# The KAN's input product on four 32-column strips, with its values copied onto the inner parts by transfers through DRAM

## The chip, the cores and the metric

The kernel runs on one core of one Trainium2 chip, as one launch. The metric is the device time of a whole execution in microseconds; the time before is 1592.74 us, the median of three runs (1592.62 to 1594.12). Besides, one execution was profiled. A core has five instruction streams that run side by side and wait for each other by semaphores: TensorE (PE, with its weight loads PEld), VectorE (DVE), ScalarE (ACT), GpSimd (POOL), and SyncE (SP), which in this kernel only issues transfers (DMAs). Each stream runs strictly in its own order: whatever waits at its head holds up all that stands behind it.

## The reference, cut to what matters

There are 16 batch rows of 512 tokens with 128 features. Six residual layers follow each other, each on the layer-normed `x`: half a KAN, causal attention with 16 heads, half a KAN, half a mixture of experts, a linear recurrence, half a mixture of experts. The change concerns the KAN, which is computed twice for each row, with the same weights, so 32 times:

```python
s = jnp.einsum('btd,dm->btm', x, Win) + bin_          # M = 64 middle features
h = jax.nn.relu(s[..., None] * W1 + b1)               # each with INNER = 16 inner functions
g = jnp.einsum('btmh,mh->btm', h, W2) + b2
out = jnp.einsum('btm,md->btd', g, Wout) + bout
```

So each of the 64 middle features is scaled, shifted and cut at zero in 16 ways, and the 16 results are added up with weights.

## The kernel before

Tokens of one row lie along the free dimension (512 of them). The 64 middle features are taken in two halves of 32. On the 128 partitions stand four copies of one half, one for each of four inner parts (partition = part times 32 + feature), and each inner part has four inner functions. One ACT instruction (`kan_h`, L377) with a scale and a bias for each partition therefore makes 4 times 32 of the relu values for all tokens; eight of them, four to a half, make all 1024.

To have the same 32 values on four groups of partitions, the kernel before keeps the input weights four times side by side (`win`, 128 x 2 x 4 x 32) and lets one 128x512 matmul per half (`ps_s`, L358) compute each value four times. ACT copies the result out of PSUM to `kan_s0` and `kan_s1` (L361). Then come the eight `kan_h`, eight matmuls of 32 output partitions (`ps_kg`, L387) which sum over the inner functions, a copy (`kan_g`, L393), the output product (`ps_ko`, L401), and the add to `x` on DVE (L402).

Buffers: `kan_s0` has two (and shares them with `kan_g` and others), `kan_s1` has one. The flag `kan_held` keeps a second KAN from writing `kan_s1` before the first has released it. Two PSUM banks, `mm`, are lent by `bank()` to all side work.

What sets the order: the kernel is a set of Python generators, which a planner steps turn by turn (`turn()`). What is emitted in one turn goes into the streams of PE, ACT, DVE and POOL in that order and stays there. Copies out of PSUM are put off to the next turn (`later`, `flush`). While `paced` is set, each turn has a budget for each engine (`MOST`), and a generator that asks for more than is left (`need`, or `bank` with its `work`) waits for a later turn. SP's order isn't written by hand: a scheduler places the transfers by when it estimates their data to be ready.

The main loop has one stage for each row (44 turns): in it `weights(b)` makes the exponentials of row b (`ps_st` L713 on PE, `pt` L716 on ACT, masks L718 on POOL), `maxima(b + 1)` the scores of the next row for their maxima (`ps_sc` L649, DVE L654 and L659), and `outputs` the product with the values (`ps_av` L739). Beside them run as side work `stage_out(b - 1)` (output product, second KAN, gate) and `stage_in(b + 4)` (first KAN, then `attn_in`, which makes the queries and keys of that row). `attn_in` writes the parts of queries and keys to DRAM (`qs` L427, `ks` L434) and reads them back onto the partitions of the scores (`qp` L516, `kp` L510); row maxima go the same way (`ms` L688, `qp` L690). All these are SP's.

Before the first stage the rows 0, 1 and 2 go through their first KAN, rows 0 and 1 through `attn_in` (`first`, `second`, `forward`), while SP loads weights and all of `x`. After the last stage come the experts (L1026, L1039, L990) with the recurrences as side work; the last two second KANs, of rows 14 and 15, run into that time.

The matmuls of fp32 are split in the records into two: a product of 512 columns shows as two instructions.

Of the kernel before, what the change touches and what calls it, by code (L numbers as in the profile page):

```python
# [8 lines left out]
F32 = mybir.dt.float32  # L9
# [8 lines left out]
P = 128  # L18
S = 512
NT = S // P  # L20
D = 128
M = 64
MH = M // 2
NI = 4
# [12 lines left out]
GB = 8  # L37
IN, OUT = 38, 8
LATE = 28
EP = 5  # L40
PLACES = 8
AHEAD = 4
# [6 lines left out]
def tile_macaron(  # L49
# [9 lines left out]
    nc = tc.nc  # L59
# [45 lines left out]
    with ExitStack() as ph:  # L105
# [17 lines left out]

        center = w1p.tile([D, D], F32, name="center", tag="yT")
        nc.vector.tensor_scalar_add(center, ident, -1.0 / D)
        win = cst.tile([D, 2, NI, MH], F32, name="win")
        binc = cst.tile([P, 2], F32, name="binc")
        kw1 = cst.tile([P, 2, NV], F32, name="kw1")
        kb1 = cst.tile([P, 2, NV], F32, name="kb1")
# [4 lines left out]
                rows = src[half * MH : (half + 1) * MH, :]  # L134
                nc.scalar.dma_start(out=dst[:, half, :], in_=rows.rearrange("m (i v) -> i m v", i=NI))

        for half in range(2):
            cols = win_in[:, half * MH : (half + 1) * MH]
            nc.sync.dma_start(out=win[:, half, :, :], in_=cols.unsqueeze(1).to_broadcast([D, NI, MH]))
        inner(kw1, kw1_in)  # L140
        for half in range(2):
            rows = bin_in[half * MH : (half + 1) * MH]
# [102 lines left out]
        def take(**work):  # L245

            for e, w in work.items():
                room[e] -= w
# [8 lines left out]
                yield  # L257

        held, kan_held, hurry = [0], [0], [False]

        def bank(shape, dtype, name, work=0.0):


            while held[0] == 2 or (paced[0] and work > room["pe"]):
                yield
            room["pe"] -= work
            held[0] += 1
            return mm.tile(shape, dtype, name=name, tag="mm")

        def freed():  # L270
            held[0] -= 1
# [26 lines left out]
        def norm(xt, name="kan_xT", pool=None, whole=False):  # L298

            st = small.tile([P, NT, 6], F32, name="ln_st")  # L300
            mv = small.tile([P, NT, 2], F32, name="ln_mv")
            for c in range(NT):
                if c % 2 == 0:
                    yield from need(dve=0.55)
                nc.vector.bn_stats(out=st[:, c, :], in_=xt[:, c, :])
            yield
            yield from need(dve=0.6, pool=1.4)
            for c in range(NT):
                nc.vector.bn_aggr(out=mv[:, c, :], in_=st[:, c, :])  # L309
            rstd = small.tile([P, NT], F32, name="ln_rstd")  # L310
            nc.gpsimd.tensor_scalar_add(rstd, mv[:, :, 1], EPS)  # L311
            nc.gpsimd.tensor_tensor(rstd, rstd, mhalf, ALU.pow)  # L312
            yield
            yield
            yield
            yield from rest(1)
            xl = w2p.tile([P, NT, D], F32, name="kan_x")
            if whole:
                for c in range(NT):
                    if c % 2 == 0:  # L320
                        yield from need(dve=0.85)
# [27 lines left out]
        def kan(b):  # L349

            _, xT = yield from norm(x[b])
            sk = []
            for half in range(2):
                while half and kan_held[0]:
                    yield
                kan_held[0] |= half
                ps = yield from bank([P, S], F32, "ps_s", 0.9)
                nc.tensor.matmul(ps, lhsT=win[:, half, :, :].rearrange("d i m -> d (i m)"), rhs=xT,  # L358
                                 start=True, stop=True)
                sh = (w1p if half else w2p).tile([P, S], F32, name=f"kan_s{half}")  # L360
                later.append(lambda sh=sh, ps=ps: nc.scalar.copy(sh, ps))  # L361
                yield
                take(act=0.6)
                freed()
                sk.append(sh)
            yield

            hs = []
            begin = now[0]
            U = 2 * NV  # L370
            for t in range(U):
                while now[0] < begin + 15 * t // 8:
                    yield
                yield from need(act=0.8, **({"pool": 1.25} if t == 1 else {}))
                half, v = t // 2 % 2, t // 4 * 2 + t % 2
                h = hp.tile([P, S], F32, name="kan_h")
                nc.scalar.activation(h, sk[half], AF.Relu, bias=rbias[:, half, v : v + 1],  # L377
                                     scale=kw1[:, half, v : v + 1])
                hs.append((half, v, h))
                if t == 1:  # L380
                    nc.gpsimd.tensor_tensor(x[b], x[b], kcst.unsqueeze(1).to_broadcast([P, NT, D]), ALU.add)
                yield
            pg = yield from bank([P, S], F32, "ps_kg", 1.0)
            for begins in (True, False):
                for half, v, h in hs[0:4] if begins else hs[4:8]:
                    o = half * M + v % 2 * MH
                    nc.tensor.matmul(pg[o : o + MH, :], lhsT=w2d[:, half, v, :], rhs=h,  # L387
                                     start=begins, stop=not begins)
                if begins:
                    yield  # L390
                    yield from need(pe=1.0)
            gT = w2p.tile([P, S], F32, name="kan_g", tag="kan_s0")
            later.append(lambda: nc.scalar.copy(gT, pg))  # L393
            kan_held[0] = 0
            yield
            take(act=0.6)
            freed()
            yield
            po = yield from bank([P, NT, D], F32, "ps_ko", 0.9)
            for c in range(NT):  # L400
# [119 lines left out]
        def centered(ps, w, to=None):  # L520

            ps = ps[:, 0 : w.shape[1]]
            nc.tensor.matmul(ps, lhsT=center, rhs=w, start=True, stop=True)
            if to is None:
                nc.vector.tensor_copy(w, ps)
            else:
                nc.vector.tensor_copy(to, ps.rearrange("k (h d) -> k d h", d=HD))

        def center_win():
            psc = yield from bank([P, 2 * NI * MH], F32, "ps_kc0")  # L530
            centered(psc, win.rearrange("d a i m -> d (a i m)"))
            freed()

        def cleared(pack):
# [777 lines left out]
```

## Time and profile before

| | |
|---|---|
| median of 3 runs | 1592.74 us (1592.62 to 1594.12) |
| profiled execution, whole time | 1585.11 us |
| its span | 1583.1 us |
| mean granted clock of PE | 0.984 |
| first scores (L649) | 67.9 us after the span's start |
| `ps_s` products (L358) | 71.1 us of PE in 128 records, 644 ns each |
| copies to `kan_s` (L361) | 64, 586 ns each |
| `kan_h` (L377) | 256, 821 ns each |
| `ps_kg` (L387) | 512 records on strips of 32 columns |
| SP's transfers in all | 67.7 MB on its queue, DMA engines busy 15% for it |

The profile has one execution, so all stretches of time below are of that one, which is 7.6 us shorter than the median. Its view of busy times gives each engine's share, which adds up to more than the span, since the engines overlap. What counts is the chain of work that ended last: it is followed back from the last instruction, at each step to what released it or to the instruction before it on its engine. Where a line has its time in that chain, shortening it shortens the whole, until something else ends last. The view of instructions in order of time shows start, duration, engine, line and count; what stands there in brackets is the idle time before an instruction and what ended it.

### The profile page before, as it was taken

The page shows a single profiled execution, that of the slowest core. Times are in us where ns is not written, and L with a number is a line of the kernel's source. Part 1 is how long each engine was busy: PE and PEld are TensorE (multiplying, and loading weights), DVE is VectorE, ACT ScalarE, POOL GpSimd, SP SyncE. Part 2 cuts the span into 40 slices and gives each one's busy share as a digit, 9 for nine tenths or more (in the row PEclk, how much of TensorE's full clock was granted, in tenths as well). Part 3 has the DMA queues.
Part 4 walks back from the last instruction along what each step waited for, and adds up shares of the span by engine and source line. Part 5 has one row for each costly group of instructions (what it writes and reads, how often), then busy time and mean ns, then how long its engine had stood idle before and what let it go on. Part 6 is the DMA issues. An engine that isn't in the chain of part 4 may idle for free.

```text
span 1583.1 us, 33175 instructions
## 1 busy us (share of the span) xinstructions
PE 1479.8 (93%) x11902; PEld 1045.6 (66%) x11905; DVE 1085.0 (69%) x3574; ACT 960.5 (61%) x1852; POOL 922.7 (58%) x1439
## 2 busy tenths in 40 slices
PE   4689989999999999999999899999999999999997
PEld 2334454455445454445444489999998999999997
DVE  5587877878788788888888345765569665753333
ACT  3445767777778777777776865444454444544443
POOL 2535545555555564556454766667666666767773
PEclk9889999999999999999999999999999999999998
DMA  5220110122111210221122113223332332333332
GB/s 136 81 58 30 58 52 13 50 59 60 36 33 53 60 52 12 58 60 35 30 79 68 50 45 70 60 57 73 72 73 59 72 72 63 81 64 67 69 67 60
DMA packets 107466, 92.87 MB, mean 59 GB/s; under 512 B 23469, under 2 KB 95862, under 8 KB 107062
## 3 DMA queue, kind: packets, MB, share of 16 engines
q1 hardware_dynamic: 84464, 67.67, 15.0%
q0 software_dynamic: 21584, 22.89, 7.8%
q8 instruction: 93, 1.52, 0.4%
q14 instruction: 71, 0.58, 0.1%
q10 hardware_dynamic: 1254, 0.20, 0.1%
HBM read 59.20 MB, written 35.45 MB: 60 GB/s over the span
## 4 chain that ended last, share of the span: by engine, by line
PE 76%; DVE 10%; ACT 7%; issue 2%; DMA 2%; POOL 1%; SPq 1%; ACTq 0%; DVEq 0%; POOLq 0%
PE ps_h L1026 13%; PE ps_y L1039 13%; PE ps_av L739 9%; PE ps_st L713 7%; PE ps_sc L649 5%; PE acc L990 5%; PE ps_kg L387 4%; ACT pt L716 4%; PE ps_s L358 3%; DVE below L654 3%; ACT kan_h L377 2%; PE ps_t L338 2%; PE ps_x L955 2%; DVE topped L659 2%; PE ps_g L800 2%
## 5 line engine op out<-in xcount | busy, mean ns | idle before, releaser
L716 ACT ACTIVATE pt<-ps_st 128x512 f32<-128x512 f32 x682 | 369.9, 566 | 126.3 <-PE ps_st L713 124.6
L718 POOL TENSOR_SCALAR_AFFINE_SELECT pt<-pt 128x128 f32<-128x128 f32 (+2 forms) x704 | 250.9, 365 | 320.4 <-ACT pt L716 314.4
L654 DVE CUSTOM_DVE_ANT_0 below<-ps_sc,causal 128x512 bf16<-128x512 f32 (+1 forms) x512 | 315.6, 616 | 106.5 <-PE ps_sc L649 91.0
L935 POOL DMA_INDIRECT xg<-xnd,tokI x256 | 252.8, 988 | 82.9 <-issue 37.8
L1028 ACT ACTIVATE mo<-ps_h 128x512 f32<-128x512 f32 x256 | 152.8, 597 | 217.7 <-PE ps_h L1026 217.4
L713 PE MATMUL ps_st<-qp,kp 128*128 128x512 bf16 (+1 forms) x990 | 247.6, 301 | 33.2 <-ACT pt L716 30.7
L1026 PE MATMUL ps_h<-xin,mw 128*128 128x128 f32 x2048 | 272.5, 276 | 0.0
L1039 PE MATMUL ps_y<-mw,mo 128*128 128x128 f32 x2048 | 270.8, 275 | 0.0
L649 PE MATMUL ps_sc<-kp,qp 96*128 96x512 bf16 (+3 forms) x1024 | 256.6, 304 | 5.9 <-DVE topped L654 3.9
L1026 PEld LDWEIGHTS ps_h<-xin,mw 128*128 128x128 f32 x2048 | 250.3, 192 | 12.4 <-issue 9.9
L1039 PEld LDWEIGHTS ps_y<-mw,mo 128*128 128x128 f32 x2048 | 249.4, 192 | 1.0 <-DVE ye L1036 0.8
L713 PEld LDWEIGHTS <-kp 128*128 128x128 bf16 x1024 | 94.9, 100 | 183.9 <-issue 164.7
L377 ACT ACTIVATE kan_h<-kan_s,rbias,kw 128x512 f32<-128x512 f32 x256 | 207.6, 821 | 0.0
L1056 POOL DMA_INDIRECT sum<-mo,tokI x93 | 152.1, 1635 | 69.7 <-issue 26.7
L739 PE MATMUL ps_av<-pt,va 128*32 128x512 f32 (+3 forms) x2048 | 164.6, 439 | 1.0 <-POOL pt L718 0.7
L649 PEld LDWEIGHTS <-qp 96*128 96x128 bf16 x1024 | 95.9, 99 | 87.4 <-issue 64.7
L659 DVE TENSOR_REDUCE topped<-ps_sc 128x2 f32<-128x512 f32 (+1 forms) x192 | 127.0, 683 | 23.1 <-PE ps_sc L649 22.8
L739 PEld LDWEIGHTS ps_av<-pt,va 128*32 128x32 f32 x2048 | 53.3, 109 | 85.4 <-issue 42.7
L312 POOL TENSOR_TENSOR ln_rstd<-ln_rstd,mhalf 128x4 f32<-128x4 f32 x96 | 102.4, 1067 | 8.0
L311 POOL TENSOR_SCALAR ln_rstd<-ln_mv 128x4 f32<-128x4 f32 x96 | 21.9, 228 | 138.1 <-DVE ln_mv L309 137.7
L1045 DVE SCALAR_TENSOR_TENSOR ye<-ps_y,gainT,ye 128x128 fp32r<-128x128 f32 x83 | 29.0, 349 | 84.7 <-ACT ye L1042 84.4
L1045 DVE SCALAR_TENSOR_TENSOR parts<-ps_y,gainT,parts 128x128 fp32r<-128x128 f32 x80 | 27.9, 349 | 83.9 <-ACT parts L1042 83.8
(204 smaller groups left out, 2296.5 us busy)
## 6 DMA issues: line engine op xcount, KB each, us to landing
qp<-qs SPq DMA_DIRECT2D x64, 288.0 KB
xnd<-kan_x SPq DMA_DIRECT2D x32, 256.0 KB
sum<-x SPq DMA_DIRECT2D x62, 128.0 KB
qs<-qpart SPq DMA_DIRECT2D x48, 128.0 KB
kp<-ks SPq DMA_DIRECT2D x48, 96.0 KB
x<-in_L_attn_x_dram SPq DMA_DIRECT2D x16, 256.0 KB
mw<-in_L_ffn_w_dram SPq DMA_DIRECT2D x16, 256.0 KB
xg<-xnd,tokI POOLq DMA_INDIRECT x256, 2.5
```

What stands on the lines that cost most here:

```text
L377: nc.scalar.activation(h, sk[half], AF.Relu, bias=rbias[:, half, v : v + 1], scale=kw1[:, half, v : v + 1])
L649: nc.tensor.matmul(v[:, u, 0:n], lhsT=qp[r][0:MXR, g, bass.ts(c, P)], rhs=kp[0:MXR, r, 0:n], start=alone, stop=(u == len(gs) - 1), skip_gr ...
L654: nc.vector.tensor_tensor_reduce(below[:, 0:n], v[:, 0, 0:n], causal[:, S - n : S], 1.0, LOWEST, ALU.add, ALU.max, accum_out=maxs[:, h, c ...
L659: nc.vector.tensor_reduce(maxs[:, h : h + len(gs), c], v[:, :, 0:n], AX.X, ALU.max)
L713: nc.tensor.matmul(v[:, u, 0:n], lhsT=kp[ROWS, r, bass.ts(c, P)], rhs=qp[r][ROWS, g, c * P : S], start=True, stop=True)
L716: nc.scalar.activation(o, v[:, :, 0:n], AF.Exp, scale=HD ** -0.5)
L718: nc.gpsimd.affine_select(out=dg, in_=dg, compare_op=ALU.is_ge, fill=0.0, base=0, pattern=[[0, len(gs)], [1, P]], channel_multiplier=-1)
L739: nc.tensor.matmul(po[32 * g : 32 * g + 32, c * P : S], lhsT=va[:, c, r, :], rhs=pt[:, g, OFF[c] : OFF[c] + n], start=(c == 0 and not odd) ...
L935: nc.gpsimd.indirect_dma_start(out=xgs[i // E % 2][:, i % E, :], out_offset=None, in_=xnd[b], in_offset=bass.IndirectOffsetOnAxis(ap=tokI[ ...
L1026: nc.tensor.matmul(pst[:, f, :], lhsT=mw1[e][:, bass.ts(f, P)], rhs=xins[i // E % 2][:, i % E, :], start=True, stop=True)
L1028: nc.scalar.activation(hs[u], pst, AF.Gelu)
L1039: nc.tensor.matmul(py, lhsT=hs[u][:, f, :], rhs=mw2[e][:, f, :], start=(f == 0), stop=(f == NF - 1))
```

## The change

`win` is kept once (128 x 64). The product is made once: four matmuls, each of 32 output partitions and 256 tokens, write the two halves of features and the two halves of tokens on four strips of one PSUM bank. ACT copies 256 columns to `kan_m`. Two transfers write it to a DRAM tile `kn` of 64 features by 512 tokens, and two transfers read from that tile, one for each half of features, four times over onto the four groups of partitions of `kan_s0` and `kan_s1`. The flag `kan_held` is taken before both reads, not between the two halves. Between the reads and the first `kan_h` the generator rests three turns (`REST`).

```diff
-        win = cst.tile([D, 2, NI, MH], F32, name="win")
+        win = cst.tile([D, M], F32, name="win")
...
+        nc.sync.dma_start(out=win, in_=win_in)
...
             _, xT = yield from norm(x[b])
+            ps = yield from bank([P, S // 2], F32, "ps_s", 0.75)
+            for half in range(2):
+                for th in range(2):
+                    o = th * M + half * MH
+                    nc.tensor.matmul(ps[o : o + MH, :], lhsT=win[:, half * MH : (half + 1) * MH],
+                                     rhs=xT[:, th * S // 2 : (th + 1) * S // 2], start=True, stop=True)
+            sm = w1p.tile([P, S // 2], F32, name="kan_m")
+            later.append(lambda: nc.scalar.copy(sm, ps))
+            yield
+            take(act=0.4)
+            freed()
+            scr = tc.dram_tile([2, MH, S], F32, name=f"kn{len(kns)}")
+            kns.append(scr)
+            for th in range(2):
+                nc.sync.dma_start(out=scr.rearrange("a m t -> (a m) t")[:, th * S // 2 : (th + 1) * S // 2],
+                                  in_=sm[th * M : (th + 1) * M, :])
+            yield
+            while kan_held[0]:
+                yield
+            kan_held[0] = 1
+            yield
             sk = []
             for half in range(2):
-                while half and kan_held[0]:
-                    yield
-                kan_held[0] |= half
-                ps = yield from bank([P, S], F32, "ps_s", 0.9)
-                nc.tensor.matmul(ps, lhsT=win[:, half, :, :].rearrange("d i m -> d (i m)"), rhs=xT,
-                                 start=True, stop=True)
                 sh = (w1p if half else w2p).tile([P, S], F32, name=f"kan_s{half}")
-                later.append(lambda sh=sh, ps=ps: nc.scalar.copy(sh, ps))
-                yield
-                take(act=0.6)
-                freed()
+                nc.sync.dma_start(out=sh, in_=scr[half].unsqueeze(0).to_broadcast([NI, MH, S]))
                 sk.append(sh)
-            yield
+            for _ in range(REST):
+                yield
```

The product that centers `win` (`center_win`) becomes 64 columns wide instead of 256.

More of the change, by code (lines that the diff above doesn't have):

```diff
@@ L39 @@
 LATE = 28
+REST = 3
 EP = 5
@@ L135, in inner @@
                 nc.scalar.dma_start(out=dst[:, half, :], in_=rows.rearrange("m (i v) -> i m v", i=NI))
-        for half in range(2):
-            cols = win_in[:, half * MH : (half + 1) * MH]
-            nc.sync.dma_start(out=win[:, half, :, :], in_=cols.unsqueeze(1).to_broadcast([D, NI, MH]))
+        nc.sync.dma_start(out=win, in_=win_in)
         inner(kw1, kw1_in)
@@ L259, in tile_macaron @@
         held, kan_held, hurry = [0], [0], [False]
+        kns = []
         def bank(shape, dtype, name, work=0.0):
@@ L351, in kan @@
             _, xT = yield from norm(x[b])
+            ps = yield from bank([P, S // 2], F32, "ps_s", 0.75)
[19 more added lines that the diff above has]
+            yield
             sk = []
             for half in range(2):
-                while half and kan_held[0]:
-                    yield
-                kan_held[0] |= half
-                ps = yield from bank([P, S], F32, "ps_s", 0.9)
-                nc.tensor.matmul(ps, lhsT=win[:, half, :, :].rearrange("d i m -> d (i m)"), rhs=xT,
-                                 start=True, stop=True)
                 sh = (w1p if half else w2p).tile([P, S], F32, name=f"kan_s{half}")
-                later.append(lambda sh=sh, ps=ps: nc.scalar.copy(sh, ps))
+                nc.sync.dma_start(out=sh, in_=scr[half].unsqueeze(0).to_broadcast([NI, MH, S]))
+                sk.append(sh)
+            for _ in range(REST):
                 yield
-                take(act=0.6)
-                freed()
-                sk.append(sh)
-            yield
             hs = []
@@ L529, in center_win @@
         def center_win():
-            psc = yield from bank([P, 2 * NI * MH], F32, "ps_kc0")
-            centered(psc, win.rearrange("d a i m -> d (a i m)"))
+            psc = yield from bank([P, M], F32, "ps_kc0")
+            centered(psc, win)
             freed()
```

## The prediction

> **What bounds the kernel now.** The page first: its chain of work that ended last, then its times by engine.
>
> ```profile
> span 1583.1 us, 33175 instructions
> PE 1479.8 (93%) x11902; PEld 1045.6 (66%) x11905; DVE 1085.0 (69%) x3574; ACT 960.5 (61%) x1852; POOL 922.7 (58%) x1439
> PE 76%; DVE 10%; ACT 7%; issue 2%; DMA 2%; POOL 1%; SPq 1%; ACTq 0%; DVEq 0%; POOLq 0%
> PE ps_h L1026 13%; PE ps_y L1039 13%; PE ps_av L739 9%; PE ps_st L713 7%; PE ps_sc L649 5%; PE acc L990 5%; PE ps_kg L387 4%; ACT pt L716 4%; PE ps_s L358 3%; DVE below L654 3%; ACT kan_h L377 2%; PE ps_t L338 2%; PE ps_x L955 2%; DVE topped L659 2%; PE ps_g L800 2%
> ```
>
> PE carries the chain, and the product that the change rewrites (ps_s, L358) lies on it with 3% of the span. Busy times by stretch say how closely PE binds during attention; columns are PE, PEld, DVE, ACT, POOL busy, granted clock, DMA share, GB/s:
>
> ```profile
> 468.00:520.00 52.00, 49.64 (x400) 25.34 (x396) 42.56 (x141) 41.29 (x77) 29.75 (x64) 1.00 0.16 46
> ```
>
> PE is busy 95%, DVE 82%, ACT 79%: what PE saves is mostly saved, until ACT or DVE takes over. DMA engines are idle 84%. The chain in order of time prices one KAN (start, us, what; x2 is one matmul, which the records split in two):
>
> ```profile
> 441.02 0.99 PE ps_av L739 x8
> 443.43 1.43 PE ps_av L739 x24
> ...
> 448.59 0.98 PE ps_s L358 x2
> ...
> 451.34 0.88 PE ps_s L358 x2
> 452.24 0.58 ACT kan_s L361
> ```
>
> Last, the instructions in order of time at the start, SP's queue and ACT (start, us, count):
>
> ```profile
> 24.28 5.70 SPq L195 DMA_DIRECT2D wo<-in_L_attn_Wo_dram  x8
> 30.08 1.17 SPq L217 DMA_DIRECT2D wlam<-in_L_attn_W_lam_dram  x2
> 31.30 0.58 SPq L219 DMA_DIRECT2D wf<-in_L_attn_W_F_dram  x1
> 31.93 1.11 SPq L1082 DMA_DIRECT2D wst<-in_L_attn_W_fromP_dram  x2
> ```
>
> ```profile
> 17.23 0.59 ACT L361 COPY kan_s<-ps_s 128x512 f32<-128x512 f32 x1 [2.17 <-PE ps_s L358]
> 18.75 0.58 ACT L361 COPY kan_s<-ps_s 128x512 f32<-128x512 f32 x1 [0.94 <-PE ps_s L358]
> 19.24 5.75 ACT L377 ACTIVATE kan_h<-kan_s,rbias,kw 128x512 f32<-128x512 f32 x8
> ```
>
> The first KAN has its input at 17-19 us, while SP issues loads until 32. Today the KAN needs nothing from SP.
>
> The sum is made against this execution: 1585.1 us, span 1583.1 and 2.0 around it. The median of the three runs shown is 1592.7, 7.6 above; I add the change to that.
>
> **The change, part by part.** There are 32 KANs (two for each of 16 batch rows). In the built orders the planner's turns are 3 more (1613 against 1610), all of them before the first scores; each attention stage keeps its 44 turns, about 1.18 us each (52 us by 44).
>
> *1. Product and copies (removed, added).* Two 128x512 products cost 0.98 + 0.88 = 1.86 us of chain. The four 32x256 products stand on four strips, as ps_av's do: eight records of 512 columns took 0.99, 24 records of 384, 256 and 128 columns 1.43, so a group of 256 about 0.48. After strip work the next ps_st stands with 0.27-0.32 in the chain instead of 0.22; I allow 0.2 for going into strips and back. PE saves 1.1-1.2 per KAN. ACT's two 0.585 copies become one of 256 columns (L957's took 0.37): 0.8 saved. 27 KANs lie in PE-bound attention stages (not the first five: three precede the scores, two fall into the stage whose pace DVE's score maxima set). PE: 27 x 1.15 = 31, of which I take 80%, since ACT and DVE are close behind: 25. ACT, on about a fifth of that stage's chain (pt 11.0%, kan_h 6.1%, copies): 27 x 0.8 x 0.18 = 4. Together **-29**; ends -38 (all of PE's, plus ACT's and the bubbles) and -15 (half of PE's).
>
> The page "TensorEngine Tiling (Array Packing)", Key Properties, of the Trainium skill speaks against this part: changing the tiling mode drains TensorE. It gives no price; the 0.05-0.1 us after strip groups above is what the chain shows of it.
>
> *2. The first KANs (a new wait).* In the built order of SP's queue the first KAN's two writes stand behind all the loads above, up to wf. So they issue at about 31.4 and 32.0 instead of the value being there at 18. Small writes land 2.0-2.3 us after issue (the trace's completion records of ks and qs), so the first broadcast read issues at 34.1; an unhurried 256 KB read lands after 2.7-3.0 (x<-sum). ACT's first kan_h: about 37 instead of 19.2. It stands at the head of ACT's queue, and PE's ps_kg behind it stands ahead of the transposes of the next two KANs, so rows 1 and 2 don't fill the gap. DVE's clearing of buffers does part of it. Then: kan(0) +14 at its add, row 0's rope +13; kan(1) may read only once kan(0) released its buffers, +12 at its end; kan(2)'s second read issues behind row 0's four query loads (4 x 288 KB and 288 KB of keys, of which the last landed 6.3 us after issue before) and lands near 75; ACT's kan_xT of row 1 stands behind the kan_h that waits for it (58.2 before, 77 now). PE's first scores follow row 1's products and kan(2)'s ps_kg and ps_ko: 67.9 before, 86 now. Nothing later has slack to take this back. **+18.5**; ends 13 (only the 13 seen at row 0's rope) and 22.
>
> *3. Steady state: do the reads come in time?* After the copy: two writes (issue about 0.55 each), 2.0 to land, a read at 2.9, there at 5.7 on idle queues. REST and the other yields place the first kan_h five turns after the copy where nothing else holds it (5.9 - 0.37 = 5.5 us), seven or more in most KANs. So most wait 0-0.3: nothing taken. Not so where SP has row b-1's query loads at that moment. In the built queue the reads of the first KANs of rows 8, 10 and 12 stand behind two key writes, three qp loads and three kp loads. Before, those took this:
>
> ```profile
> 478.46 0.54 SPq L434 DMA_DIRECT2D ks<-kpart  x1
> 479.37 0.82 SPq L516 DMA_DIRECT2D qp<-qs  x1
> 480.58 2.06 SPq L510 DMA_DIRECT2D kp<-ks  x3
> 482.68 1.58 SPq L516 DMA_DIRECT2D qp<-qs  x2
> 484.46 0.39 SPq L797 DMA_DIRECT2D xnd<-kan_x  x1
> ```
>
> Counted from the copy: last key write (it waits for POOL's last part) 3.0, qp to 5.2, kp to 7.2, the read at 7.2; behind such loads the xnd above landed 5.4 us after issue, so 12.3. ACT stands 12.3 - 5.5 = 6.8. Behind it stand the exponentials, so POOL's masks, ps_av and, once both ps_st banks are full, all of PE: about 1 us of run-ahead, 5.8 lost. 3 x 5.8 = **+17.5**; ends 9 (the read lands in 3, two turns run ahead) and 24.
>
> The skill's "DMA: Bandwidth & Descriptors", Anatomy of one DMA, has about 2.0 us plus bytes by 436 GB/s for a DMA. By it the 256 KB read takes 2.6, not 5.4; these stalls would be 3.3 each, part 3 ten, and the whole sum +6.5 instead of +14. The page prices a DMA alone; the xnd row had other loads ahead of it, and I go by the row.
>
> *4. Other places on SP.* The second KANs of rows 12 and 13 have two expert-weight loads ahead of their reads, which wait for PE two to four turns: 2.5 and 4 late, less run-ahead 4.5. Row 14's first KAN stands behind one query and one key write: 1. The last KAN falls among the experts, where turns are shorter (0.8 us: the combines of one row follow those of the last after 19 us and 24 turns): 1.5 lost, its 1.1 gained. **+7**; ends 0 and 15.
>
> *At nothing.* DMA volume: 640 KB per KAN, two in 52 us, +25 GB/s on the 46 shown, covered by the 84% idle share. SP: 2.2 us of issue and some 2 of waiting per KAN; behind it queue xnd (first gathered at 886), row maxima and query loads used a stage later. Without that distance each would cost the same 4 us. The narrower input weights shorten an early product and two loads; the start waits for SP's later loads anyway. Recurrences, routing and experts keep their turns.
>
> Sum: -29 + 18.5 + 17.5 + 7 = **+14**: 1599 as profiled, 1607 against the median.
>
> **Rivals.**
> - *The reads come in time* (ends faster). Place: rows 8, 10, 12. If ACT runs late enough, or the reads pass the loads, part 3 is nothing: -29 + 18.5 + 7 = -3.5, 1589. It decides once the three stalls together are under 3.5. For it: ACT is idle a fifth of the stage, and kan_h may simply be reached later; against it: 6.8 us is more than the idle of five turns (1.2). With PE's saving at its upper end too it is 1580.
> - *Nearly every KAN waits.* If reads take 4.5-5.5, as qp<-qs does in the trace, instead of 2.9, every KAN five to seven turns out loses about 1 more: 27 x 1 = +27, 1634. For it: the margin is below 0.3 in the five-turn KANs. Against: most have seven turns, and queues are idle then.
> - *PE doesn't speed up* (the strips don't run side by side, or ACT becomes the bound): part 1 at -10, 1626. ps_av and ps_kg groups speak against it.
>
> **How the numbers follow.** No change that this kernel's runs can tell is about 0.2%, 3.2 us. Forecast (slower, 1597-1622) 0.5; reads in time or PE's saving whole 0.27, of which 0.06 within 3.2 us of the median; nearly every KAN waits 0.13; PE not faster 0.1. The bounds added all good give -16, all bad +46; leaving out 0.2 at the outside: 1586 to 1632. Faster 0.23, same 0.07, slower 0.7.
>
> **What would show it.** Right: first kan_h near 37, first ps_sc near 86, ps_s in groups of 8 records of about 0.5, stages 1-2 us shorter except those of rows 8, 10, 12, ACT there waiting 5-7 us for a DMA into kan_s before kan_h. Wrong: first scores before 80; no ACT wait above 3 us; or short DMA waits before most kan_h.

## The result, and the profile after

The changed kernel takes 1704.97 us (median of 4 runs, 1700.41 to 1709.88) against 1592.68 us (4 runs) for the kernel before on the same chip: 1.0707 times as long, 95% interval 1.068 to 1.0734. The prediction was 1607, range 1586 to 1632: the direction is right, and the loss is 112 us instead of 14. The profiled execution of the changed kernel took 1704.2 us, span 1702.3, so it stands for the median.

The page after: span, busy times, and the chain of work that ended last, by engine and by line.

```profile
span 1702.3 us, 33567 instructions
PE 1482.3 (87%) x12029; PEld 1043.9 (61%) x12033; DVE 1087.4 (64%) x3574; ACT 940.8 (55%) x1820; POOL 921.2 (54%) x1439
PE 62%; DMA 16%; DVE 8%; ACT 8%; SPq 2%; issue 2%; POOL 1%; ACTq 0%; DVEq 0%; POOLq 0%
PE ps_h L1039 12%; PE ps_y L1052 12%; DMA kan_s<-kn 11%; PE ps_av L752 6%; PE ps_st L726 5%; PE acc L1003 4%; PE ps_sc L662 4%; ACT kan_h L390 3%; ACT pt L729 3%; PE ps_kg L400 3%; DVE below L667 3%; PE ps_t L338 3%; DMA kn<-kan_m 2%; PE ps_x L968 2%; PE ps_g L813 1%
```

DMA had 2% of the chain and now has 16%, 11% of it the broadcast reads (`kan_s<-kn`, 186 us) and 2% the writes. The product itself has left the list; its PE time fell from 71.1 us to 21.8. And yet PE is busy as long as before (1482.3 against 1479.8): what the product saved came back as slower matmuls, of which more below. The rest of the span's 119 us is PE idle.

Who waited for whom (us in total, times, longest), first ACT's own waits, then PE's:

```profile
ACT kan_h L390 <- DMA kan_s<-kn: 151.8, 43, 23.2
```

```profile
PE ps_st L726 <- ACT pt L729: 102.8, 78, 10.7
```

The first wait did not exist before. The second is its echo: while ACT stands at `kan_h`, the exponentials behind it don't run, PE finds both `ps_st` banks taken and stops. In the kernel before the same line was

```profile
PE ps_st L713 <- ACT pt L716: 30.7, 66, 0.9
```

and it is back at 29.0 us in the first experiment below, where nobody waits for the reads. KAN by KAN the first `kan_h` waits 0.4 to 5.4 us in nearly every row, 8.9 in row 3, and 9.3, 10.0 and 9.6 us in the first KANs of rows 8, 10 and 12. Row 8 in order of time (start, us, what; in brackets the idle time before and what ended it):

```profile
427.42 1.20 SPq L366 DMA_DIRECT2D kn<-kan_m  x2
428.72 0.56 SPq L447 DMA_DIRECT2D ks<-kpart  x1
429.80 0.85 SPq L529 DMA_DIRECT2D qp<-qs  x1
430.72 0.54 SPq L447 DMA_DIRECT2D ks<-kpart  x1
431.32 1.70 SPq L529 DMA_DIRECT2D qp<-qs  x2
...
434.05 2.08 SPq L523 DMA_DIRECT2D kp<-ks  x3
436.17 1.14 SPq L376 DMA_DIRECT2D kan_s<-kn  x2
...
442.49 0.81 ACT L390 ACTIVATE kan_h<-kan_s,rbias,kw 128x512 f32<-128x512 f32 x1 [9.33 <-DMA kan_s<-kn]
...
443.73 0.48 PE L726 MATMUL ps_st<-qp,kp 128*128 128x384 bf16 x1 [10.03 <-ACT pt L729]
```

The reads stand on SP behind two key writes, three `qp` and three `kp` loads, as the prediction had it. They issue 8.1 us after the second write and land 6.3 later. PE's 10.03 us are not all that it costs. Busy time by stretch around it (PE, PEld, DVE, ACT, POOL busy, granted clock of PE, DMA share, GB/s):

```profile
430.00:433.00 3.00, 3.00 (x35) 1.50 (x34) 1.80 (x6) 0.95 (x3) 1.50 (x3) 1.00 0.34 109
433.00:443.00 10.00, 0.61 (x3) 0.19 (x2) 3.16 (x14) 0.67 (x2) 0.29 (x1) 0.75 0.52 156
443.00:445.00 2.00, 0.99 (x4) 0.38 (x4) 0.44 (x1) 2.00 (x5) 1.25 (x2) 0.50 0.22 75
445.00:447.00 2.00, 2.00 (x11) 1.67 (x10) 1.11 (x7) 1.48 (x4) 1.92 (x5) 0.50 0.05 12
447.00:449.00 2.00, 2.00 (x16) 1.47 (x15) 0.80 (x2) 1.59 (x4) 0.89 (x3) 0.67 0.00 0
449.00:451.00 2.00, 2.00 (x17) 1.30 (x19) 1.97 (x5) 2.00 (x5) 0.93 (x2) 1.00 0.34 92
```

During the wait the granted clock falls to a half, and it is back at 1.00 some 5 us after PE has work again: at 445 to 449 PE is fully busy at 0.5 to 0.67. The mean over the span fell from 0.984 to 0.948. (The Trainium skill's "TensorE: Matmul & The Clock Gate", Part 1, says so: half the clock after an idle window of about 3.4 us, the full one after a busy window. The trace agrees: PE has next to no work from 433 on, and its clock records show a half from 438.1 to 448.3. The prediction did not price it.)

The start, in order of time:

```profile
15.88 0.37 ACT L359 COPY kan_m<-ps_s 128x256 f32<-128x256 f32 x1 [1.20 <-PE ps_s L356]
...
31.24 1.11 SPq L366 DMA_DIRECT2D kn<-kan_m  x2
33.88 1.20 SPq L376 DMA_DIRECT2D kan_s<-kn  x2
39.48 1.52 ACT L390 ACTIVATE kan_h<-kan_s,rbias,kw 128x512 f32<-128x512 f32 x2 [23.23 <-DMA kan_s<-kn]
...
102.03 0.81 PE L662 MATMUL ps_sc<-kp,qp 96*128 96x512 bf16 x3
```

The value is on chip at 16.3, and ACT gets it at 39.5. The first scores come at 102.0 instead of 67.9.

The trace's completion records say how long a transfer took from issue to landing. The two reads of a KAN land 5.4 and 7.6 us after issue (medians), and the quickest of the first ones 4.8. Such a read shows five completion events: one after 1.0 us, the other four close together just before it has landed. Writes of 64 KB (`kn`), 2.0 us, show 16.

### The profile page after: what moved, and what is told of

Same layout as the page of the kernel before. It is cut to its first block, busy times and chain, and to the rows that moved or that the text cites. A ratio compares the mean times of both kernels' runs of the same rounds, so it can differ in the third digit from the quotient of the medians.

```text
span 1702.3 us, 33567 instructions
## 1 busy us (share of the span) xinstructions
PE 1482.3 (87%) x12029; PEld 1043.9 (61%) x12033; DVE 1087.4 (64%) x3574; ACT 940.8 (55%) x1820; POOL 921.2 (54%) x1439
## 4 chain that ended last, share of the span: by engine, by line
PE 62%; DMA 16%; DVE 8%; ACT 8%; SPq 2%; issue 2%; POOL 1%; ACTq 0%; DVEq 0%; POOLq 0%
PE ps_h L1039 12%; PE ps_y L1052 12%; DMA kan_s<-kn 11%; PE ps_av L752 6%; PE ps_st L726 5%; PE acc L1003 4%; PE ps_sc L662 4%; ACT kan_h L390 3%; ACT pt L729 3%; PE ps_kg L400 3%; DVE below L667 3%; PE ps_t L338 3%; DMA kn<-kan_m 2%; PE ps_x L968 2%; PE ps_g L813 1%
## 5 line engine op out<-in xcount | busy, mean ns | idle before, releaser
L729 ACT ACTIVATE pt<-ps_st 128x512 f32<-128x512 f32 x682 | 365.7, 561 | 136.6 <-PE ps_st L726 134.1
L726 PE MATMUL ps_st<-qp,kp 128*128 128x512 bf16 (+2 forms) x988 | 259.0, 315 | 104.8 <-ACT pt L729 102.8
L948 POOL DMA_INDIRECT xg<-xnd,tokI x256 | 253.1, 989 | 80.5 <-issue 37.4
L390 ACT ACTIVATE kan_h<-kan_s,rbias,kw 128x512 f32<-128x512 f32 x256 | 207.0, 815 | 155.0 <-DMA kan_s<-kn 151.8
L662 PE MATMUL ps_sc<-kp,qp 96*128 96x512 bf16 (+3 forms) x1024 | 270.2, 318 | 9.6 <-DVE topped L667 7.9
L662 PEld LDWEIGHTS <-qp 96*128 96x128 bf16 x1024 | 100.3, 103 | 153.4 <-issue 128.5
L752 PE MATMUL ps_av<-pt,va 128*32 128x512 f32 (+3 forms) x2048 | 170.6, 452 | 0.2 <-POOL pt L731 0.2
L400 PE MATMUL ps_kg<-kan_h,w2d 128*32 128x512 f32 x512 | 77.6, 621 | 23.4 <-ACT kan_h L390 20.0
L338 PE MATMUL ps_t<-ident,kan_x 128*128 128x128 f32 x384 | 66.0, 302 | 29.4 <-DVE kan_x L326 21.3
```

The costliest lines, as they stand in the source:

```text
L662: nc.tensor.matmul(v[:, u, 0:n], lhsT=qp[r][0:MXR, g, bass.ts(c, P)], rhs=kp[0:MXR, r, 0:n], start=alone, stop=(u == len(gs) - 1), skip_gr ...
L726: nc.tensor.matmul(v[:, u, 0:n], lhsT=kp[ROWS, r, bass.ts(c, P)], rhs=qp[r][ROWS, g, c * P : S], start=True, stop=True)
L729: nc.scalar.activation(o, v[:, :, 0:n], AF.Exp, scale=HD ** -0.5)
L752: nc.tensor.matmul(po[32 * g : 32 * g + 32, c * P : S], lhsT=va[:, c, r, :], rhs=pt[:, g, OFF[c] : OFF[c] + n], start=(c == 0 and not odd) ...
L948: nc.gpsimd.indirect_dma_start(out=xgs[i // E % 2][:, i % E, :], out_offset=None, in_=xnd[b], in_offset=bass.IndirectOffsetOnAxis(ap=tokI[ ...
```

## The experiments

The runs fell on several chips. From the experts' first product to the end the profiled kernels take 665 to 669 us on two of them, 678 to 682 on one and 703 to 714 on two, whichever kernel it is; what comes before agrees better (the changed kernel reaches that product at 1033.8 and, on a chip of the last kind, at 1035.0). So beside each ratio to the kernel before on the same chip (1.01 is 1% longer; the 95% interval in brackets), I give that moment ("experts begin"; before 917.9 and 926.2). The ratio of one and the same kernel is not the same on every chip either: the changed one has 1.0707 and 1.0789, the strips without transfers 0.9999 and 0.9959. So differences between ratios of different chips are good to 0.4 to 0.8%, 6 to 13 us.

**Is it the waiting, or the load?** ACT reads a constant instead of `kan_s`, first with the transfers, then without (the writes and reads are left out).

```diff
-                nc.scalar.activation(h, sk[half], AF.Relu, ...)
+                nc.scalar.activation(h, rope[:, half, :], AF.Relu, ...)
```

> Leaves out the use of the product: kan_h reads a constant table instead of kan_s; the strip product, its copy, the writes and the reads are all still made, but nobody waits for the reads. Theory 'late values' (the loss is waiting for the values, and TensorE's clock at 0.5 after each wait; the saving on PE is real): no wait for kan_s, granted clock back to about 0.98, first scores near 70, time 1555 to 1575, below the kernel before. Rival 'the transfers cost by themselves' (SP's queue and the DMA engines delay other transfers, or strips save PE nothing): 1600 or more.

> Leaves out the use of the product, as the run with a constant table for kan_h, and the writes and reads too: strip product and its copy alone. The difference to that run is what the transfers cost as load. Theory 'late values': within 6 us of it. Rival 'the transfers cost by themselves': faster than it by 20 us or more.

Measured: 1.0043 (1.0017 to 1.007) with the transfers, 0.9999 (0.9981 to 1.0018) without. Experts begin at 927.2 and 920.7. So nearly all of the loss (1.0707 to 1.0043) is waiting for the values: the same writes and reads, with nobody waiting, cost 0.4%, some 7 us, and in the four stages of rows 6 to 9 nothing (207 us with them and without). Counted to the moment when the experts begin it is the same: 107 us of waiting (1033.8 against 927.2) and 6.5 of load. Of the 107, 27.5 are there at the first scores (102.0 against 74.5), and the rest comes in the stages. But the other half of the expectation failed. Without any waits the kernel was to be 20 to 35 us faster than before, and it is not faster at all. Two things were open: why the reads come so late, and where the saving went.

**Why the reads take 5 to 8 us.** The copies of one feature are put on neighbouring partitions, so that the read's outermost dimension has 32 entries instead of 4. Bytes, number and order stay.

```diff
-    nc.sync.dma_start(out=sh, in_=scr[half].unsqueeze(0).to_broadcast([NI, MH, S]))
+    nc.sync.dma_start(out=sh, in_=scr[half].unsqueeze(1).to_broadcast([MH, NI, S]))
...
-    nc.scalar.dma_start(out=dst[:, half, :], in_=rows.rearrange("m (i v) -> i m v", i=NI))
+    nc.scalar.dma_start(out=dst[:, half, :], in_=rows.rearrange("m (i v) -> (m i) v", i=NI))
```

> Edit: the copies of a feature stand on neighbouring partitions (partition = feature times 4 + part), so that the outermost dimension of a broadcast read has 32 entries instead of 4; weights and biases of the inner functions are laid out to match; size, number and order of the transfers stay. Theory 'four lanes' (a transfer is spread over DMA engines by its outermost dimension, and a read with 4 entries there uses few of them): the reads land about 3 us after issue instead of 5.3 and 7.6, the waits of 1 to 5 us before kan_h (24 KANs, some 57 us) nearly vanish, the three of 9 to 10 us in rows 8, 10, 12 shrink to about 6, first scores 2 to 4 us earlier than 101.9; time 1620 to 1650. Rival 'a read of 256 KB through DRAM takes that long anyway': landing stays at 5 us and more, time within 15 us of 1705.

Measured: 1.0395 (1.0345 to 1.0445), first scores at 93.6, experts begin at 983.1, 51 us sooner than with four entries. The two reads land 3.0 and 3.3 us after issue (medians), with 16 completion events each. In the chain that ended last, the first KAN's read stands in the changed kernel and in this one as (start, us):

```profile
33.88 5.51 DMA kan_s<-kn
```

```profile
33.50 2.99 DMA kan_s<-kn
```

ACT's waits, of which the changed kernel had 151.8 us in 43:

```profile
ACT kan_h L390 <- DMA kan_s<-kn: 89.2, 17, 20.8
```

What is left are the start (20.8 and others), 8.9, 7.8 and 8.5 in rows 8, 10 and 12, 7.3 in row 3, and the last four KANs (2 to 4 each). Of the common waits of 1 to 3 us most are gone. So the time of a read went with the shape of its outermost dimension, not with its bytes: which axis is stretched, with the weights laid out to match, made 3% of the kernel. The gain is a little smaller than expected (1.0395 is 1656 us on the first chip, and 1620 to 1650 was expected), though the first scores came 8 us earlier instead of 2 to 4. The three rows hardly moved: there the wait is for SP's turn, and behind the key and query loads even these reads took 4.6 to 5.7 us.

**The start.** The KANs of rows 0, 1 and 2 go by the wide product.

```diff
+            if kans[0] < OLD:                 # OLD = 3
+                kans[0] += 1
+                sk = yield from wide(xT)      # as in the kernel before
+            else:
+                sk = yield from strips(xT)    # as in the changed kernel
```

> The first three KANs (rows 0, 1, 2, before the first scores) are made by the wide product of the kernel before, all others as in the changed kernel. Theory 'the start adds in full' (the 34 us by which the first scores are later, 101.9 against 67.9, come back later nowhere): first scores at 68 to 71, time about 1705 - 34 = 1671 (1660 to 1680). Rival 'later stages would wait anyway' (the late start is partly covered): 1685 or more.

Measured: 1.0607 (1.0561 to 1.0653). The first scores come at 68.4, 34 us sooner, but the experts begin only 17 us sooner (1017.1). In the stages between, ACT waits 8 us longer for `kan_s`, and PE is busy for 12 us more for the same instructions, at a lower clock. So about half of the start's delay was regained later, which is the rival's case (1.0607 is 1689 us on the first chip). Why the waits grow again there is open.

**Where the saving went.** For this the product was measured by itself, without transfers and with a constant table for `kan_h`, in four ways: wide with the turns of rest, on strips with them, on strips without them, and on strips with the rest and a row's first KAN begun three turns earlier. Beside them stands the kernel before.

The wide product in the changed kernel's frame:

```diff
-            ps = yield from bank([P, S // 2], F32, "ps_s", 0.75)
...
+            for half in range(2):
...
+                ps = yield from bank([P, S], F32, "ps_s", 0.9)
+                nc.tensor.matmul(ps, lhsT=win[:, half, :, :].rearrange("d i m -> d (i m)"), rhs=xT,
+                                 start=True, stop=True)
...
+                later.append(lambda sh=sh, ps=ps: nc.scalar.copy(sh, ps))
...
+            for _ in range(1 + REST):
+                yield
```

The strips without rest, and, with it, begun earlier (`IN` is the turn of a stage at which the first KAN of the row four further on starts):

```diff
-REST = 3
+REST = 0
```

```diff
-IN, OUT = 38, 8
+IN, OUT = 35, 8
```

> The kernel before, profiled on the chip of the three runs beside it, to compare stages on one chip. Expected: the attention part (up to the experts' first product) ends near 918 us as in the first profile; if the chip is the slower kind, the difference is in the experts alone (665 us before).

> Leaves out the use of the product (kan_h reads a constant table). The two wide products and their two copies as in the kernel before, with as many turns to the first kan_h as in the changed kernel, no transfers. The partner of the next run. Theory 'saving as forecast' and rival 'saving not taken' alike: within 8 us of the kernel before, since nothing waits for the copies anyway.

> The strip product and its copy without transfers, kan_h on a constant table (a repeat, now beside the wide product in the same frame). Theory 'saving as forecast' (part 1 of the prediction): 25 to 29 us less than with the wide product. Rival 'saving not taken' (the time that PE saves turns into PE idle, since the stage's pace is set by PE and ACT waiting for each other): 0 to 12 us less, with PE's busy time down by 20 or more and its idle time up.

> Leaves out the use of the product (kan_h on a constant table) and the transfers, and the rest of three turns too: strip product and copy alone, with the KAN's first kan_h in the same turn of its stage as in the kernel before (turn 13 of 44; 15 in the changed kernel). So only part 1 of the prediction is left. Theory 'the later turns ate it' (the two turns by which the KAN stands later in its stage cost what PE saves; with the wide product the same frame cost 45 us): 20 to 29 us below the kernel before. Rival 'the pace is set by PE and ACT waiting for each other' (less work on PE becomes idle time of PE): 5 to 12 us below, as with the three turns.

> Leaves out the use of the product (kan_h on a constant table) and the transfers, keeps the rest of three turns, but a row's first KAN is begun three turns earlier in its stage (turn 35 of the stage before instead of 38), so that its first kan_h stands in turn 12 of 44, as in the kernel before (12 or 13), instead of 13 or 15. Theory 'the KAN stands too late in its stage' (the 1.5% by which the rest of three turns is slower come from the place, not from the number of turns): at least half of the gain is back, 1.2 to 1.9% below the kernel before. Rival 'the turns between product and kan_h cost by themselves' (buffers held longer, the second KAN still late): 0 to 0.6% below, as with the rest and the late start.

The sums of busy time over the four stages of rows 6 to 9 (eight KANs), us and then the engines: the kernel before; wide with rest; strips with rest; strips without rest; strips with rest, begun earlier.

```profile
sum 210.00, PE 199.15 PEld 102.90 DVE 169.14 ACT 161.35 POOL 118.08; mean PE 49.79 PEld 25.73 DVE 42.29 ACT 40.34 POOL 29.52
```

```profile
sum 225.00, PE 203.55 PEld 102.26 DVE 172.65 ACT 161.96 POOL 116.37; mean PE 50.89 PEld 25.56 DVE 43.16 ACT 40.49 POOL 29.09
```

```profile
sum 207.00, PE 191.59 PEld 98.52 DVE 171.46 ACT 155.83 POOL 116.96; mean PE 47.90 PEld 24.63 DVE 42.86 ACT 38.96 POOL 29.24
```

```profile
sum 202.00, PE 190.39 PEld 98.46 DVE 168.83 ACT 156.25 POOL 117.67; mean PE 47.60 PEld 24.61 DVE 42.21 ACT 39.06 POOL 29.42
```

```profile
sum 204.00, PE 193.24 PEld 98.60 DVE 173.45 ACT 156.84 POOL 116.98; mean PE 48.31 PEld 24.65 DVE 43.36 ACT 39.21 POOL 29.25
```

| kernel | ratio to before (95%) | first scores | experts begin |
|---|---|---|---|
| before | 1 | 69.4 | 926.2 |
| wide, rest | 1.0286 (1.0273 to 1.03) | 77.5 | 974.0 |
| strips, rest | 0.9959 (0.9944 to 0.9974) | 72.7 | 916.8 |
| strips, no rest | 0.9809 (0.9784 to 0.9835) | 69.3 | 900.1 |
| strips, rest, begun earlier | 0.9881 (0.9863 to 0.99) | 72.3 | 898.3 |

Strips without rest against before: PE busy 8.8 us less over eight KANs, and 8 us less time. So a KAN's saving is 1.0 us and is taken nearly whole. (No run has the wide product in its own place with the constant table, so a part of this can be that nobody reads `kan_s`.) The three turns of rest take most of it back: PE is about as little busy (191.6), but the four stages take 5 us more, nearly 4 of them PE idle. The frame matters even more where the work is wider: the old product in it is 2.9% slower than in its own place, against an expectation of no change, and so strips and wide product differ by 52 us in this frame, where 25 to 29 were forecast. The saving can't be read from that pair.

Then the earlier start tells why. It keeps the rest and moves the KAN to its old place in the stage (turn 12 of 44 for the first `kan_h`, instead of 13 or 15), and from the first scores to the experts it needs 826 us: as few as without rest (831), against 844 with rest and the late place. From POOL's first mask of row 2 to that of row 14 the five kernels of the table take 632, 671, 622, 607 and 605 us, in the table's order. So in the stages the cost is the place and not the number of turns. By the whole time only half of the 1.5% is back (0.9881, against 0.9809 without rest). The start (72.3 against 69.3) keeps its part of the rest; the remainder is no larger than what two chips differ by for one kernel, so these runs don't show whether it is real.

**The clock.** The changed kernel again, and with useless products in PE's stream where it stands idle in rows 8, 10 and 12.

```diff
+                if t == 0 and n in (12, 16, 20) and held[0] < 2:
+                    pf = yield from bank([P, S], F32, "ps_f")
+                    for _ in range(8):
+                        nc.tensor.matmul(pf, lhsT=ident, rhs=rope[:, 0, :], start=True, stop=True)
+                    freed()
```

> The changed kernel again, on the chip of the runs beside it: 7% above the kernel before.

> The changed kernel, with eight useless 128x512 products (about 0.98 us each, 7.8 in all) put into PE's stream right behind the first kan_h of rows 8, 10 and 12, where PE stands idle for 10 us in the trace and its granted clock is 0.5 for about 10 us afterwards. Theory 'the clock is part of the loss' (idle PE loses its clock; kept busy it does not): granted clock after these three waits stays at 1.0, and the time is 8 to 15 us below the changed kernel, though PE does 23 us more work. Rival 'only the wait counts': within 3 us of the changed kernel, or above it.

The changed kernel was 1.0789 (1.0758 to 1.0819) on this chip, the filled one 1.081 (1.0776 to 1.0844): no difference. Busy time by stretch around row 8's wait, first without, then with the filling:

```profile
432.00:442.00 10.00, 1.41 (x14) 0.60 (x7) 3.33 (x14) 0.49 (x1) 0.29 (x1) 0.66 0.53 164
442.00:446.00 4.00, 1.68 (x7) 0.87 (x7) 0.86 (x6) 3.20 (x6) 1.95 (x4) 0.50 0.20 69
446.00:460.00 14.00, 14.00 (x115) 7.42 (x114) 9.92 (x28) 11.44 (x22) 5.49 (x15) 0.90 0.13 36
```

```profile
438.00:448.00 10.00, 8.19 (x31) 3.62 (x23) 3.19 (x14) 0.49 (x1) 0.29 (x1) 1.00 0.48 143
448.00:452.00 4.00, 1.73 (x7) 0.95 (x7) 1.09 (x8) 2.75 (x6) 2.04 (x5) 0.75 0.38 127
452.00:466.00 14.00, 14.00 (x122) 7.60 (x121) 9.95 (x28) 12.34 (x24) 5.45 (x15) 0.95 0.12 36
```

PE kept busy does keep its clock: 1.00 instead of 0.66 in the wait, and 3.4 us at half speed after each of the three waits instead of 10.2 to 13.7. That the time didn't follow speaks against the clock as a large part of the loss in these rows, or the filling cost as much as it gave; the run doesn't tell these apart.

**Versions meant to be faster than both.** Wide product for the first KANs of rows 0 to 4, 32-entry reads, and for rows 8, 10 and 12 the reads on ACT's queue:

```diff
+                queue = nc.scalar if n in (12, 16, 20) else nc.sync
+                queue.dma_start(out=sh, in_=scr[half].unsqueeze(1).to_broadcast([MH, NI, S]))
```

> A version meant to beat both: first KANs of rows 0 to 4 by the wide product, the others on strips with broadcast reads of 32 outermost entries, and the reads of the first KANs of rows 8, 10, 12 issued on ACT's queue instead of SP's, so that they don't stand behind query and key loads. Theory 'late values are the whole loss' with 'saving as forecast': first scores at 68 to 70, no wait for kan_s above 3 us, 15 to 25 us below the kernel before. With 'saving not taken': between 8 us below and 5 above it.

Measured: 1.0083 (1.007 to 1.0096), first scores at 67.8. ACT's wait in rows 8, 10, 12 fell to 1.7, 3.5 and 1.1, all waits of the stages together to 22.2 us. So these repairs took back 6% of the 7%, and the kernel is still slower than before: 13 us, outside of both expectations.

```diff
-            if n < OLD:
+            if n in (0, 1, 2, 3, 4, 12, 16, 20, 28, 29, 30, 31):
                 sk = yield from wide(xT)
```

> The wide product for the KANs whose values came late on strips (rows 0 to 4 first; rows 8, 10, 12 first; the last four), strips with reads of 32 outermost entries for the other 20. Theory 'late values are the whole loss': no wait for kan_s above 1.5 us, 3 to 10 us below the kernel before. Rival 'the later turns and the loads cost as much as PE saves': between 3 us below and 8 above it.

With wide products for those three and for the last four KANs as well (and no reads on ACT's queue): 1.0105 (1.0073 to 1.0137), no better, and both expectations missed. The long waits had moved: 6.4, 5.9 and 5.9 us, now in the first KANs of rows 9, 11 and 13.

The version with reads on ACT's queue again, with `IN` at 35 and at 34:

> The version with the wide product for the first five KANs, reads of 32 outermost entries and three KANs' reads on ACT's queue, and a row's first KAN begun three turns earlier in its stage. Theory 'the KAN stands too late': 0.5 to 1.2% below the same version without the earlier start (which was 0.8% above the kernel before), so at the kernel before or under it. Rival 'the turns cost by themselves': 0.5 to 1% above the kernel before, unchanged.

> The same, begun four turns earlier: the first kan_h of a row's first KAN stands in turn 9 instead of 12. Theory 'the KAN stands too late': no better than three turns earlier, within 0.4% of it. Rival 'the turns cost by themselves': 0.5 to 1% above the kernel before.

Measured: 1.0034 (1.002 to 1.0047) and 0.9965 (0.9952 to 0.9978). The first is 0.5% below the same version without the earlier start, the least that the theory of the place had foreseen. It has long waits of the same make in rows 9 and 11 (7.6 and 9.1 us), here row 9 in order of time:

```profile
416.46 1.12 SPq L418 DMA_DIRECT2D kn<-kan_m  x2
417.68 1.47 SPq L480 DMA_DIRECT2D ks<-kpart  x2
419.26 1.67 SPq L562 DMA_DIRECT2D qp<-qs  x2
421.04 2.05 SPq L556 DMA_DIRECT2D kp<-ks  x3
423.14 1.21 SPq L429 DMA_DIRECT2D kan_s<-kn  x2
...
428.24 0.81 ACT L371 ACTIVATE kan_h<-kan_s,rbias,kw 128x512 f32<-128x512 f32 x1 [7.58 <-DMA kan_s<-kn]
```

With four turns the reads pass ahead of these loads in all rows but one (15, 7.2 us):

```profile
ACT kan_h L371 <- DMA kan_s<-kn: 41.4, 21, 7.2
```

This last version (1595.1 us against 1601.0 on its chip) is the only one with the values through DRAM that beats both kernels, the kernel before by a third of one per cent. It does not confirm the theory of the place: that had a start four turns earlier as no better than three, and it was 0.7% better, because the reads passed the loads. And it is not shown to be the strips' gain, for no run begins the kernel before, with its wide product, as many turns earlier.

## Why the prediction was wrong, step by step

Right sign, wrong size. In us of this kernel, predicted and as the runs have it, once by the ratios of the whole time and once by the moment when the experts begin:

| step | predicted | by whole time | by the experts' beginning |
|---|---|---|---|
| 1. product and copies | -29 | -30 (0.9809) | -26 (900.1 against 926.2) |
| rest and later place ("at nothing") | 0 | +24 to +30 (0.9959 and 0.9999, against 0.9809) | +17 to +21 (916.8 and 920.7) |
| transfers as load ("at nothing") | 0 | +7 (1.0043 against 0.9999) | +6.5 (927.2 against 920.7) |
| 2., 3. and 4., waits for the values | +43 | +106 (1.0707 against 1.0043) | +107 (1033.8 against 927.2) |

All but the load compare runs of different chips, so each of these is good to some 6 to 13 us.

*Step 1* held, in size and kind: 1.0 us per KAN, where the sum had 1.07 (25 + 4 over 27). The "four strips" ran side by side: a group of eight records of 256 columns takes 0.64 us in all, where 0.48 and an allowance of 0.2 were foreseen. So the rival "PE doesn't speed up" is out.

*Step 2.* The queue was read rightly to the tenth: writes at 31.2 (31.4 foreseen), read at 33.9 (34.1). The step that failed is the next: "an unhurried 256 KB read lands after 2.7-3.0 (x<-sum)". It landed after 5.5, and the second after 7.5. The first `kan_h` came at 39.5 instead of 37; row 2's second read, foreseen to land near 75, was issued at 80.5 and landed 9.4 us later. The first scores came at 102 instead of 86. With the old product for these three rows about half of the 34 us came off the end, so "nothing later has slack to take this back" was too strong, too.

*Step 3* has the decisive error, and it is the same one: the read "there at 5.7 on idle queues", and with it "So most wait 0-0.3: nothing taken". From copy to `kan_h` it took about 8 to 10 us in common KANs, where the value was foreseen after 5.7; some 2.5 us of that are the read. The three rows were the right ones, and by the right mechanism: 9.3, 10.0, 9.6 us instead of 6.8 (the read issued 9.6 to 9.8 after the copy instead of 7.2, and landed after 6.3 to 6.9 instead of 5.4; besides, the prediction's 12.3 is a slip, since 7.2 and 5.4 make 12.6). From POOL's first mask of one row to that of the next, the three stages with these stalls take 10.3, 11.3 and 10.6 us longer than where nobody waits, 32 in all instead of 17.5. So of the 107 us up to the experts' beginning the start has 27.5 (18.5 foreseen), these three stages 32, and all the other waits 47, where step 4 had 7. The other rows' 1 to 5 us each make up more: of ACT's 100.7 us of waits between the first scores and the experts, 29 are these three. So the rival "nearly every KAN waits" was the true case, and by its own words ("If reads take 4.5-5.5"), but its price of 1 us per KAN was too small. A warning was in the trace before: `qp<-qs`, also a stretched read, of 288 KB and with 24 entries in its outermost dimension, shows 13 completion events and took 3.5 to 6.3 us. And the key write `ks<-kpart`, with 4 entries there, shows five events, though its 32 KB land in 2.0 us. No row of before has both the size and the shape of the new read. I went by `x<-sum`, which has as many bytes, but 16 events. The Trainium skill's "DMA: Bandwidth & Descriptors", Rules for kernel authors, had the point and I passed it over: a leading stretched dimension of c copies confines a transfer to at most c of the engines. The run with 32 entries agrees with it: 3.0 us instead of 5.4 for the same bytes. The figure that the prediction quotes from that page (2.6 for 256 KB) comes near what the spread read took, and is half of what the narrow one took. (The page gives it for transfers issued by GpSimd; these are SP's.)

*Step 4.* The last four KANs wait 4.1, 5.4, 5.4 and 3.2 us and row 14's first one 2.5; foreseen were 7 in all.

*At nothing.* The volume was rightly put at next to nothing: with nobody waiting, the transfers cost some 7 us. The larger miss is not in the list, but in the sentence "each attention stage keeps its 44 turns": it does, and what is done in them shifts by one to two turns. With the rest at the start this costs 17 to 30 us, more than half of what the product saves, or all of it.

*Not in the sum:* PE's clock. Over the stages PE is busy for 788.0 us in the changed kernel and for 764.8 with the same matmuls and no waits, 23 us more. Whether these 23 are on the path is open: filling three of the waits gave the clock back, and no time. The two rows, from the first scores to the experts (us, then PE, PEld, DVE, ACT, POOL busy, granted clock, DMA share, GB/s), the changed kernel first:

```profile
102.00:1033.80 931.80, 788.02 (x6264) 399.09 (x6267) 665.96 (x2188) 596.75 (x1117) 456.10 (x982) 0.93 0.22 64
```

```profile
74.40:920.70 846.30, 764.81 (x6265) 384.18 (x6268) 665.12 (x2188) 592.75 (x1117) 454.25 (x979) 0.97 0.18 49
```

## What to carry to other kernels

Price a transfer by a row of the same shape, not only of the same size: look first at how many entries its outermost dimension has, above all where a broadcast puts a small one there, and count the completion events of the nearest rows. If work is put behind a round trip through DRAM, begin it as many turns earlier as the trip takes; to let it stand later "within the same number of turns" is not free. And when a wait is taken out of one row, look at what the queue does in the next: here the same stall moved on to the neighbouring rows twice.

## What the runs showed of the hardware that was not expected

- A 256 KB read from DRAM with a stretched outermost dimension of 4 landed 5.4 us after issue, the next one behind it 7.6; with 32 entries 3.0 and 3.3. Its completion events number 5 and 16.
- PE idle for 10 us is at half its clock for 10.2 to 13.7 us counted from within the wait, so that the first 5 us of work run slowly; with PE kept busy for 7 of the 10 it is 3.4 us.
- Between chips the part of gathers, experts and scatters differs by up to 45 us (665 to 669 against 703 to 714 us), while the attention part of one kernel agrees within 10.
